# Graph attention with residual and row norm on one core: moving the finish of one late block, and merging two early stores

## The chip, the cores and the metric

The kernel runs on one core of one Trainium2 chip. The metric is the device time in microseconds (us) from the start to the end of one execution. Before the change it is 244.12 us, the median of 4 runs that lie between 243.44 and 244.42 us.

## The reference

`x` is 4096 x 512, `adj` is 4096 x 4096, and there are H = 4 attention heads with a weight W of 512 x (4 * 512).

```python
ht = (h @ W).reshape(N, N_HEADS, N_HIDDEN).transpose(1, 0, 2)
src = jnp.einsum('hnd,hd->hn', ht, a_src)
dst = jnp.einsum('hnd,hd->hn', ht, a_dst)
e = jax.nn.leaky_relu(src[:, :, None] + dst[:, None, :], SLOPE) + adj_mat[None]
att = jax.nn.softmax(e, axis=-1)
h_prime = jnp.einsum('hij,hjd->hid', att, ht)
...
x = _layernorm(x + h_prime.mean(axis=0), axis=-1)
```

The entries of `adj` are zero or reach up to 1e9, so in each row the largest entry outweighs all others in the softmax, as long as it leads the second largest by more than the scores can differ. The attention of a row is then 1 at one column j, and the row's result is the layer norm of `x[i] + x[j] @ mean_h(W_h)`.

## The kernel before

**Work and tiles.** The function `leading_rows` does all of the work in the usual case. Row number `p * 32 + ib` of the matrix is partition `p` of block `ib`, so the 4096 rows make NB = 32 blocks of 128 rows. All of `x` (later the result) is kept in one tile, `hold`, of 128 x 32 x 512 floats. The loop `for t in range(NB)` loads block t of `adj` (2 MB) five steps ahead, takes the maxima of 64 segments of 64 columns on VectorE (DVE), has GpSimd (POOL) fetch the leading segment by an indirect DMA (`lead`), finds the leading column in it two steps later (L193), and has POOL fetch the row of `x` at that column by another indirect DMA (`y`, L181). Three steps later TensorE (PE) transposes this row block (`turn`), ScalarE (ACT) copies it out of PSUM, and PE multiplies it by the mean of the four head weights (`products`, L221) on top of the residual. ACT takes the sum and the sum of squares (`stats`), and two blocks at a time are normalised (`rstd`, then `finish`, L261).

**Three kinds of blocks.** With Q = 4, LATE is 28 and BEHIND is 24. Blocks 0 to 23 are finished inside the loop and held in `hold`; their stores wait until all loads are issued. Blocks 24 to 27 are put by without their residual in a free `adj` buffer (`put_by`), and their `x` is added after the loop (`add_x`). Blocks 28 to 31 come through by the latest data: 28, 29 and 30 by `finish_last`, 31 by `finish_in_halves`. `finish_last(ib, True)` is one chain: DVE adds the residual (L294), takes statistics (L297) and aggregates them (L299), ACT takes the square root (L301), DVE the reciprocal (L302), and DVE scales the block (L303). `rstd_late(26..27)` is a chain for the factors of two blocks: DVE multiply-add (L254), ACT square root (L255), DVE reciprocal (L256) and DVE multiply (L257); then ACT applies the factors in `finish(26)` and `finish(27)` (L261). `finish_in_halves(31)` has two statistics on DVE (L279), an aggregate (L281), a square root on ACT (L283), a reciprocal (L284) and two scalings (L286).

**What sets the order.** The kernel is written under `manual_schedule`: each engine carries out its instructions in the order in which the program lists them, and waits at each for what it needs. The order after the loop (L443 to L492) is written out by hand. Loads of `x`, loads of `adj` and stores all go through the SyncE (SP) queue, in order; each DMA of SP also waits until the one eight places earlier has landed. The indirect DMAs go through POOL's queue, on the same 16 DMA engines. At the end, `report` puts a flag of bad rows in `any_bad` (L393), and all engines branch on it past a general path that isn't taken here.

Of the kernel before, what the change touches and what calls it, by code (L numbers as in the profile page):

```python
# [26 lines left out]
def gat_resnorm_kernel(  # L27
# [29 lines left out]
    any_bad = keep.tile([1, 1], I32, name="any_bad")  # L57

    leading_rows(tc, x, adj, W, a, out, ident, v, n_bad, any_bad)

    flag = nc.values_load(any_bad[0:1, 0:1], min_val=0, max_val=N)
# [5 lines left out]
def leading_rows(ctx, tc, x, adj, W, a, out, ident, v, n_bad, any_bad):  # L67
# [8 lines left out]
    nc = tc.nc  # L76
    N, D = x.shape
    H = a.shape[0]
    KB, NB, S = D // P, N // P, N // E
    AHEAD = 5  # L80
    Q = 4
    PIECES = 4
    LATE = NB - Q
    BEHIND = LATE - Q
# [30 lines left out]
    def load_x(lo, n):  # L115
        nc.sync.dma_start(hold[:, ds(lo, n), :], x_rows[:, ds(lo, n), :])
# [135 lines left out]
    def rstd_late(i):  # L252

        nc.vector.tensor_scalar(sd[:, i], sd[:, i], 1.0 / D, EPS, op0=OP.mult, op1=OP.add)  # L254
        nc.scalar.activation(sd[:, i], sd[:, i], AF.Sqrt)  # L255
        nc.vector.reciprocal(sd[:, i], sd[:, i])  # L256
        nc.vector.tensor_mul(nm[:, i], nm[:, i], sd[:, i])  # L257

    def finish(ib):
        i = slice(ib, ib + 1)  # L260
        nc.scalar.activation(hold[:, ib, :], o_ps.pop(ib), AF.Identity, bias=nm[:, i], scale=sd[:, i])  # L261
# [6 lines left out]
    def products_of_half(ib, k):  # L268
        for kb in range(KB):
            nc.tensor.matmul(  # L270
                o_ps[ib][k], yt_of[ib][:, kb, :], w_sum[:, kb, ts(k, D // 2)],
                start=False, stop=(kb == KB - 1),
            )
# [16 lines left out]
    def finish_last(ib, residual):  # L290

        o = o_ps.pop(ib)
        if residual:
            nc.vector.tensor_add(hold[:, ib, :], o, hold[:, ib, :])  # L294
            o = hold[:, ib, :]
        st = small.tile([P, nc.vector.BN_STATS_DIM], F32, name="st", bufs=2)
        nc.vector.bn_stats(st, o)  # L297
        mv = small.tile([P, nc.vector.BN_AGGR_DIM], F32, name="mv", bufs=2)
        nc.vector.bn_aggr(mv, st)  # L299
        r = small.tile([P, 1], F32, name="r", bufs=2)  # L300
        nc.scalar.activation(r, mv[:, 1:2], AF.Sqrt, bias=eps)  # L301
        nc.vector.reciprocal(r, r)  # L302
        nc.vector.tensor_scalar(hold[:, ib, :], o, mv[:, 0:1], r, op0=OP.subtract, op1=OP.mult)  # L303

    def store(queue, lo, n):
        queue.dma_start(out_rows[:, ds(lo, n), :], hold[:, ds(lo, n), :])
# [93 lines left out]
    for t in range(NB):  # L400
# [24 lines left out]
        ib = t - PROJECT  # L425
# [16 lines left out]

    for ib in range(BEHIND, NB, 2):  # L443
        load_x(ib, 2)
    for ib in range(0, BEHIND, 2):
        store(nc.sync, ib, 2)
    find_column(NB - 2)
    find_column_in_row(NB - 1)
# [33 lines left out]
    products(NB - 2, KB - 1, KB)  # L482
    products_of_half(NB - 1, 0)
    products_of_half(NB - 1, 1)
    rstd_late(slice(BEHIND + 2, LATE))
    finish_last(NB - 2, True)
    finish(BEHIND + 2)
    finish(BEHIND + 3)
    for ib, n in ((NB - 4, 1), (NB - 3, 1), (BEHIND, 2), (NB - 2, 1), (BEHIND + 2, 2)):
# [156 lines left out]
```

## Time and profile before

| What | Value |
|---|---|
| Time, median of 4 runs | 244.12 us (243.44 to 244.42) |
| The profiled execution's own time | 245.29 us |
| Its span, first to last instruction | 243.7 us |
| Mean granted TensorE clock | 0.941 |
| Busy: PE, DVE, ACT, POOL | 201.3, 189.1, 112.1, 96.2 us |
| DMA | 97.73 MB, mean 401 GB/s |
| Stores of two blocks (512 KB), issue to landing, median | 11.8 us |
| Stores of one block (256 KB), issue to landing, median | 2.9 us |

A line of the timeline gives the start of an instruction in us from the start of the span, its duration in us, its engine, its line in the kernel, its operation, what it writes and reads, and, in brackets, how long the engine sat idle before it and what released it. "SPq" is an instruction that issues a DMA. An engine overlaps two of its own instructions a little where neither waits for the other.

### The profile page before, as it was taken

To read this page: it belongs to the slowest core of one execution; us is meant where nothing else is said; L and a number is where in the kernel's file an instruction comes from. 1 tells how busy PE (TensorE), PEld (TensorE's weight loads), DVE (VectorE), ACT (ScalarE), POOL (GpSimd) and SP (SyncE) were. 2 spreads that over 40 slices of the span, in tenths; PEclk is the share of its full clock that TensorE was granted. 3 is DMA by queue.
4 is the path that set the end of the run, shared out by engine and by line. 5 is a ranking of instruction groups with operands and counts; after the bars stand their busy time and mean duration, and the time that the engine had idled before them with its cause. 6 is when DMAs were issued, how large, how long until landed. Compare 5 with 4: busy or idle time off the path is not lost.

```text
span 243.7 us, 2510 instructions
## 1 busy us (share of the span) xinstructions
PE 201.3 (83%) x679; PEld 104.1 (43%) x679; DVE 189.1 (78%) x312; ACT 112.1 (46%) x270; POOL 96.2 (39%) x209
## 2 busy tenths in 40 slices
PE   0198959999999999999959979599949988887950
PEld 0034514755555555555424433243323434433540
DVE  2635785589679886999589969895999999979553
ACT  2002002255656565656645555337524663183961
POOL 1112322334625643645254636363546474441100
PEclk9999776999999999999988999889986999999995
DMA  6999999999999999999999999999999999999944
GB/s 243 432 420 422 420 433 414 427 426 416 420 422 423 407 434 417 425 408 437 415 425 416 428 426 416 416 423 420 424 415 403 408 406 407 411 414 415 383 154 175
DMA packets 14993, 97.73 MB, mean 401 GB/s; under 512 B 2296, under 2 KB 2296, under 8 KB 10240
## 3 DMA queue, kind: packets, MB, share of 16 engines
q1 hardware_dynamic: 11376, 88.09, 87.2%
q0 software_dynamic: 3584, 9.44, 9.8%
q8 instruction: 6, 0.10, 0.2%
q14 instruction: 11, 0.09, 0.1%
q10 hardware_dynamic: 16, 0.02, 0.0%
HBM read 89.15 MB, written 8.39 MB: 400 GB/s over the span
## 4 chain that ended last, share of the span: by engine, by line


## 5 line engine op out<-in xcount | busy, mean ns | idle before, releaser
L158 DVE TENSOR_REDUCE seg<-adj_t 128x32 f32<-128x2048 f32 (+1 forms) x74 | 146.3, 1987 | 38.4 <-DMA adj_t<-in_adj_dram 38.2
L221 PE MATMUL o<-w_sum,yt 128*128 128x512 f32 x248 | 118.9, 621 | 4.2 <-ACT yt L210 4.2
L221 PEld LDWEIGHTS o<-w_sum,yt 128*128 128x128 f32 x248 | 46.5, 198 | 59.9 <-issue 46.6
L210 ACT COPY yt<-tp 128x512 f32<-128x512 f32 x32 | 18.8, 588 | 50.5 <-PE tp L208 50.4
L181 POOL DMA_INDIRECT y<-in_x_dram,col x32 | 30.8, 962 | 18.0 <-POOL col L195 14.6
L171 POOL DMA_INDIRECT lead<-in_adj_dram,row x32 | 32.2, 1006 | 14.2 <-POOL row L169 14.2
L311 PE MATMUL o<-hold,ident 128*128 128x512 f32 x32 | 22.1, 856 | 15.7 <-DMA hold<-in_L_gnn_W_dram 15.7
L208 PE MATMUL tp<-ident,y 128*128 128x128 f32 x128 | 20.0, 280 | 10.4 <-DMA y<-in_x_dram,col 10.4
L214 PE MATMUL o<-hold,ident 128*128 128x512 f32 x48 | 26.2, 629 | 0.0
L208 PEld LDWEIGHTS tp<-ident,y 128*128 128x128 f32 x128 | 15.2, 143 | 21.5 <-issue 21.4
L195 POOL TENSOR_TENSOR col<-start,within 128x1 uint32<-128x1 uint32 x31 | 5.9, 190 | 46.6 <-DVE within L193 46.6
L329 ACT COPY wt<-tp 128x512 f32<-128x512 f32 x16 | 9.2, 588 | 31.4 <-PE tp L327 31.4
L169 POOL TENSOR_TENSOR row<-at,first 128x1 uint32<-128x1 uint32 x32 | 6.1, 190 | 41.0 <-DVE at L167 41.0
L311 PEld LDWEIGHTS o<-hold,ident 128*128 128x128 f32 x32 | 8.4, 275 | 26.9 <-POOL row L169 11.4
L228 ACT ACTIVATE sq<-hold 128x512 f32<-128x512 f32 x32 | 19.8, 620 | 0.0
L335 PEld LDWEIGHTS pv<-at_d,wt 128*128 128x128 f32 x128 | 16.3, 191 | 6.8 <-ACT wt L329 4.0
L312 ACT ACTIVATE w_sum<-o 128x512 f32<-128x512 f32 x4 | 2.4, 597 | 35.3 <-PE o L311 35.3
L261 ACT ACTIVATE hold<-o,nm,sd 128x512 f32<-128x512 f32 x24 | 17.3, 771 | 0.0
L245 ACT ACTIVATE sq<-o,nm 128x512 f32<-128x512 f32 x24 | 16.5, 688 | 0.8
L335 PE MATMUL pv<-at_d,wt 128*128 128x2 f32 x128 | 15.3, 244 | 0.6 <-ACT wt L329 0.6
L243 ACT ACTIVATE sq<-o 128x512 f32<-128x512 f32 x24 | 14.6, 608 | 0.0
L327 PEld LDWEIGHTS tp<-ident,hold 128*128 128x128 f32 x64 | 7.9, 142 | 7.1 <-issue 7.1
(87 smaller groups left out, 135.5 us busy)
## 6 DMA issues: line engine op xcount, KB each, us to landing
adj_t<-in_adj_dram SPq DMA_DIRECT2D x27, 2048.0 KB, 32.5
adj_t<-in_adj_dram SPq DMA_DIRECT2D x20, 512.0 KB, 12.0
out_dram<-hold SPq DMA_DIRECT2D x14, 512.0 KB, 11.8
hold<-in_x_dram SPq DMA_DIRECT2D x6, 1024.0 KB, 33.7
hold<-in_L_gnn_W_dram SPq DMA_DIRECT2D x4, 1024.0 KB, 17.7
hold<-in_x_dram SPq DMA_DIRECT2D x4, 512.0 KB, 11.9
out_dram<-hold SPq DMA_DIRECT2D x4, 256.0 KB, 2.9
lead<-in_adj_dram,row POOLq DMA_INDIRECT x32, 6.2
```

What stands on the lines that cost most here:

```text
L158: nc.vector.tensor_reduce(seg_of[ib][:, ts(k, S // n)], adj_t[ib][:, ts(k, N // n)].rearrange("p (s e) -> p s e", e=E), axis=AX.X, op=OP.max,)
L171: nc.gpsimd.indirect_dma_start(out=lead, out_offset=None, in_=adj_segs, in_offset=bass.IndirectOffsetOnAxis(ap=row[:, :1], axis=0),)
L181: nc.gpsimd.indirect_dma_start(out=y, out_offset=None, in_=x, in_offset=bass.IndirectOffsetOnAxis(ap=col[:, :1], axis=0),)
L208: nc.tensor.transpose(tp[:, kb, :], y[:, ts(kb, P)], ident)
L210: nc.scalar.copy(yt, tp)
L214: nc.tensor.matmul(o_ps[ib], ident, hold[:, ib, :], start=True, stop=False)
L221: nc.tensor.matmul(o_ps[ib], yt_of[ib][:, kb, :], w_sum[:, kb, :], start=(start and kb == 0), stop=(kb == KB - 1),)
L228: nc.scalar.activation(sq, hold[:, ib, :], AF.Square, accum_out=xx[:, ib : ib + 1])
L245: nc.scalar.activation(sq, o, AF.Square, bias=nm[:, i], accum_out=sd[:, i])
L261: nc.scalar.activation(hold[:, ib, :], o_ps.pop(ib), AF.Identity, bias=nm[:, i], scale=sd[:, i])
L311: nc.tensor.matmul(o, ident, hold[:, w_at + kb * H + h, :], start=(h == 0), stop=(h == H - 1))
L335: nc.tensor.matmul(pv[:, kb, h : 2 * H : H], wt[:, k, :], at_d[:, k, h : 2 * H : H], start=(k == 0), stop=(k == KB - 1),)
```

## The change

There are two edits, both in the part after the loop. In the first, blocks 0 to 3 are stored by one DMA of 1 MB in place of two of 512 KB. In the second, the instructions of `finish_last(30)` are listed ahead of those of `rstd_late(26..27)`, in place of after them. The order of the stores stays as it is.

```diff
     for ib in range(BEHIND, NB, 2):
         load_x(ib, 2)
-    for ib in range(0, BEHIND, 2):
+    store(nc.sync, 0, Q)
+    for ib in range(Q, BEHIND, 2):
         store(nc.sync, ib, 2)
...
     products_of_half(NB - 1, 0)
     products_of_half(NB - 1, 1)
+    finish_last(NB - 2, True)
     rstd_late(slice(BEHIND + 2, LATE))
-    finish_last(NB - 2, True)
     finish(BEHIND + 2)
     finish(BEHIND + 3)
```

## The prediction

> **What bounds the kernel now.** First the page's second part. For most of the span the DMA engines are full, and the last slices are not: there the end hangs on a chain of small steps. The page's chain of waits is empty for this run, so I follow the chain by hand in the timeline.
>
> ```profile
> DMA  6999999999999999999999999999999999999944
> GB/s 243 432 420 422 420 433 414 427 426 416 420 422 423 407 434 417 425 408 437 415 425 416 428 426 416 416 423 420 424 415 403 408 406 407 411 414 415 383 154 175
> DMA packets 14993, 97.73 MB, mean 401 GB/s; under 512 B 2296, under 2 KB 2296, under 8 KB 10240
> ```
>
> Both edits lie in the last 38 us. The timeline of DVE at the end (start, duration, line, idle time before):
>
> ```profile
> 232.08 0.14 DVE L393 TENSOR_SCALAR any_bad<-total 1x1 int32<-1x1 f32 x1
> 233.98 0.17 DVE L254 TENSOR_SCALAR sd<-sd 128x2 f32<-128x2 f32 x1 [1.75 <-ACT sq L245]
> 234.41 0.17 DVE L256 RECIPROCAL sd<-sd 128x2 f32<-128x2 f32 x1 [0.27 <-ACT sd L255]
> 234.61 0.16 DVE L257 TENSOR_TENSOR nm<-nm,sd 128x2 f32<-128x2 f32 x1
> 234.69 0.69 DVE L294 TENSOR_TENSOR hold<-o,hold 128x512 f32<-128x512 f32 x1
> 235.42 0.69 DVE L297 BATCH_NORM_STATS2 st<-hold 128x6 f32<-128x512 f32 x1
> 236.15 0.18 DVE L299 BATCH_NORM_AGGREGATE mv<-st 128x2 f32<-128x6 f32 x1
> 236.69 0.16 DVE L302 RECIPROCAL r<-r 128x1 f32<-128x1 f32 x1 [0.36 <-ACT r L301]
> 236.89 0.55 DVE L303 TENSOR_SCALAR hold<-hold,mv,r 128x512 f32<-128x512 f32 x1
> 237.35 0.76 DVE L279 BATCH_NORM_STATS2 st<-o 128x6 f32<-128x256 f32 x2
> 238.14 0.21 DVE L281 BATCH_NORM_AGGREGATE mv<-st 128x2 f32<-128x12 f32 x1
> 238.72 0.16 DVE L284 RECIPROCAL r<-r 128x1 f32<-128x1 f32 x1 [0.36 <-ACT r L283]
> 238.91 0.99 DVE L286 TENSOR_SCALAR hold<-o,mv,r 128x256 f32<-128x256 f32 x2
> ```
>
> DVE stands for 1.75 us, because L254 waits for ACT's sums of block 27; from there to 239.90 it is DVE's chain that ends last. ACT beside it:
>
> ```profile
> 233.76 0.19 ACT L245 ACTIVATION_READ_ACCUMULATOR sq<-hold,nm 128x1 f32 x1
> 234.18 0.20 ACT L255 ACTIVATE sd<-sd 128x2 f32<-128x2 f32 x1 [0.23 <-DVE sd L254]
> 236.36 0.29 ACT L301 ACTIVATE r<-mv,eps 128x1 f32<-128x1 f32 x1 [1.98 <-DVE mv L299]
> 236.56 1.50 ACT L261 ACTIVATE hold<-hold,nm,sd 128x512 f32<-128x512 f32 x2
> 238.39 0.29 ACT L283 ACTIVATE r<-mv,eps 128x1 f32<-128x1 f32 x1 [0.32 <-DVE mv L281]
> ```
>
> ACT is idle for 1.98 us ahead of block 30's root, and finish(26), finish(27) are queued behind that root, though their factors are there at 234.77. The store of block 31 is issued next:
>
> ```profile
> 239.94 0.33 SPq L306 DMA_DIRECT2D out_dram<-hold  x1
> ```
>
> From that issue to the end of the span are 243.7 - 239.94 = 3.76 us (the landing and the closing barrier).
>
> Two rows of the stage before it matter for the merged store: the DMA load where the held blocks are stored (busy time of PE, PEld, DVE, ACT and POOL, granted clock, DMA share, GB/s), and the wait of PE for block 30's rows.
>
> ```profile
> 206.00:218.00 12.00, 10.54 (x31) 4.90 (x30) 10.55 (x18) 5.00 (x13) 4.94 (x11) 1.00 1.03 412
> ```
>
> ```profile
> 224.10 0.63 PE L208 MATMUL tp<-ident,y 128*128 128x128 f32 x4 [1.44 <-DMA y<-in_x_dram,col]
> ```
>
> **The moved finish, step by step.** It adds and removes no instruction. I place each start by the distances above: L294 to L297 and L297 to L299 are 0.73 each, L299 to L301 0.21, L301 to L302 0.33, L302 to L303 0.20, L254 to L255 0.20, L254 to L256 0.43, L256 to L257 0.20. An instruction that waits for nothing starts 0.07 to 0.10 before the end of the one ahead of it.
>
> - L294 follows L393, which ends at 232.22: 232.15. Its operand is there: PE's last product of block 30 ends at 231.1 (the timeline has two of 0.59, from 230.10 on). L297 232.88, L299 233.61.
> - L301 is wanted at 233.82. ACT's sums of block 27 end at 233.95, so it starts at about 233.85. The cover fits almost exactly: the wait costs 0.03.
> - L302 234.18, L303 234.38 to 234.93.
> - L254, now behind these, 234.84 (before: 233.98, so 0.86 later); L255 235.04, L256 235.27, L257 235.47 to 235.63.
> - finish(26), freed by L257, 235.66; finish(27) 0.71 later, 236.37 to 237.17 (before: to 238.07).
> - Block 31's statistics follow L257 at once: 235.54, 1.81 earlier than 237.35. PE ends its halves at 234.7, so they don't wait. L281 is 0.79 later, 236.33.
> - Block 31's root L283 is wanted 0.25 later, at 236.58, but on ACT it is now behind finish(27), which is what is late next: it starts 0.10 before that ends, 237.07. The new wait is 0.49; DVE waits for it, and so does the last store.
> - L284 237.40, L286 237.59 to 238.58, store of block 31 at 238.62: 239.94 - 238.62 = 1.32 us earlier.
>
> Of DVE's 1.81 us, ACT's queue takes 0.49. Bounds: 1.81 if the root should not have to wait, and 1.1 if the small waits at L301, L254 and L283 come out 0.2 dearer together.
>
> The moved step issues no DMA; its store is still the fourth of the last six, now issued at about 234.95 (before: 237.47), ahead of the one of blocks 26 and 27 at 237.19. That 512 KB take 1.27 us at 412 GB/s, and the last store comes 1.43 us after it, so it finds the queue free as it does now (1.85 us). If that cover failed, it would cost 0.2. SP's and POOL's other instructions keep their places. The 3.76 us behind the last issue stay.
>
> **The merged store.** One DMA issue of SP (0.33 us) goes. At 206 SP waits for landings, not for issue time, so this is worth 0. The queue is full: share 1.03, 412 GB/s. The Trainium skill (DMA: Bandwidth & Descriptors, section Bandwidth) advises at least 1 MiB per DMA, and by its fit (2.0 us and bytes at 436 GB/s) two of 512 KB would take 6.4 us and one of 1 MB 4.4: 2.0 us gained, by a transfer that stands alone. Here eight are in flight, and the row shows no gap to fill, so I take 0. Each of the next seven stores waits for a landing one place earlier in the queue and is issued 1 to 2 us sooner; the engines still serve the bytes in the same order, and all loads are ahead of the stores.
>
> There is a rule against the change. The same page (section Queues, rings and completion order) says that a DMA engine takes turns between its queues packet by packet, so a gather waits for one whole packet of SP's queue at each turn. Packet sizes can be read from the page: 14993 - 10240 = 4753 packets have 8 KB or more, and that is 27 adj loads x 128 rows, ten 1 MB loads x 128, and 17 packets of code (the queues' lines list 6 and 11). So a four-block DMA moves in 8 KB packets, a two-block one in 4 KB. At 412 GB/s over 16 engines these are 318 and 159 ns. The merged store is due on the engines at about 213 to 219, where `lead` of block 30 is in flight: issued 209.10, it landed at 214.75, and DVE sat 1.17 us waiting for it. Behind it hang block 30's `y`, issued 216.03, PE's 1.44 us of waiting and the whole end. A `lead` transfer has one row and one semaphore write per engine: at most two turns, each 0.16 longer, 0.32. By the rows, nearest first: `lead` takes 5.6 us among 4 KB packets (206 to 218) and 6.2 as the page's median, mostly among 16 KB packets, so 0.6 for 12 KB more and 0.2 for 4 KB more. The engine that lands last is then still at the 4 KB loads ahead of the store, so I take 0.1, with 0 and 0.35 as bounds. By the 1 MB rule the sum would be -1.3 - 2.0 = -3.3, by the turns rule at its worst -1.0; by the rows -1.32 + 0.1 = -1.2.
>
> **Sum.** The profiled execution would take 245.29 - 1.2 = 244.1 us, with a span of 242.5. Median: 244.12 - 1.2 = 242.9. The profiled run is 1.17 above the median; what makes it longer (if it is block 30's `y`, which took 7.9 us against 6.4 for the one before it) is ahead of all that moves, so the difference should carry over.
>
> **The rivals.**
> - *The gain is swallowed in the ACT queue.* If finish(27) or the root behind it comes 0.7 or more later than placed (a wait for factors, a collision of the last two stores), the gain is below 0.6 and the time is 243.5 to 244.2. Against it: every distance was taken from these same instructions. Chance 0.14.
> - *The merged store delays the gathers.* One mechanism: larger packets in the turns at 213 to 222 delay `lead` and then `y` of block 30. Dearest price by rows: `lead` 6.2 instead of 5.6, and `y` 8.3 (its median over the kernel, mostly among 16 KB packets) instead of 6.4, on top of what `y` of block 30 loses already, together 2.5 us, net 244.1 - 1.3 + 2.5 = 245.3. It is slower by over 0.3% once the delay is over 1.3 + 0.73 = 2.0 us. Against it: the merged DMA is only 8 packets per engine, done by 219, while `y` of block 30 is on the engines after 220. Chance 0.06.
> - *The reorder only exchanges places*, because DVE's chain is as long as before. Against it: the 1.75 us stand empty in the trace and L294's inputs are there. This would be 244.1 and is within the first rival's chance.
>
> **Numbers.** Likeliest, 0.80: 242.9, by its bounds (1.8 to 0.8 gained) 242.3 to 243.3. A measurement tells 0.3%, 0.73 us, from no change: faster means below 243.4, slower above 244.9. Range for 8 in 10, with the spread of the medians (the runs before lie 1 us apart): 242.2 to 243.7. Faster 0.80, same 0.14, slower 0.06.
>
> **What would show it.** Right: L294 of block 30 within 0.1 us after L393; L254 about 0.9 later relative to L393; L301 without a long wait; L283 starting as finish(27) ends, some 0.5 us after L281's end; the last store 6.5 us after L393 instead of 7.86. For the merge: DMA share still about 1 from 206 to 218, `lead` of block 30 still at 5.6 us. Wrong: a wait ahead of L294; PE waiting for `y` of block 30 clearly longer than 1.44 us; or a span that ends over 4 us after the last store's issue.

## The result and the profile after

The changed kernel takes 243.29 us as the median of its runs, the kernel before 244.2 us in the same comparison: a ratio of 0.9962 (95% interval 0.9945 to 0.998), which is 0.9 us less (0.5 to 1.3). The forecast was 1.2 us less. Its profiled execution has a span of 241.0 us, 2.7 us less than that of before. But 1.42 us of these lie ahead of L393, the first row of the timeline below, and are not the change's doing; the last section says where they come from.

DVE at the end of the changed kernel (the timeline's columns as before):

```profile
230.66 0.14 DVE L393 TENSOR_SCALAR any_bad<-total 1x1 int32<-1x1 f32 x1
230.74 0.69 DVE L294 TENSOR_TENSOR hold<-o,hold 128x512 f32<-128x512 f32 x1
...
232.94 0.55 DVE L303 TENSOR_SCALAR hold<-hold,mv,r 128x512 f32<-128x512 f32 x1
233.41 0.16 DVE L254 TENSOR_SCALAR sd<-sd 128x2 f32<-128x2 f32 x1
233.90 0.17 DVE L256 RECIPROCAL sd<-sd 128x2 f32<-128x2 f32 x1 [0.33 <-ACT sd L255]
234.10 0.16 DVE L257 TENSOR_TENSOR nm<-nm,sd 128x2 f32<-128x2 f32 x1
234.18 0.75 DVE L279 BATCH_NORM_STATS2 st<-o 128x6 f32<-128x256 f32 x2
234.96 0.21 DVE L281 BATCH_NORM_AGGREGATE mv<-st 128x2 f32<-128x12 f32 x1
236.03 0.16 DVE L284 RECIPROCAL r<-r 128x1 f32<-128x1 f32 x1 [0.86 <-ACT r L283]
236.23 0.99 DVE L286 TENSOR_SCALAR hold<-o,mv,r 128x256 f32<-128x256 f32 x2
```

Block 30's addition starts 0.08 us after the flag, with no wait. The idle 1.75 us of before are gone, and L254 waits for nothing. The one new stall is 0.86 ahead of L284 (0.36 before). Its cause is in ACT's timeline of the same run:

```profile
232.43 0.28 ACT L301 ACTIVATE r<-mv,eps 128x1 f32<-128x1 f32 x1
233.66 0.20 ACT L255 ACTIVATE sd<-sd 128x2 f32<-128x2 f32 x1 [0.95 <-DVE sd L254]
234.29 1.52 ACT L261 ACTIVATE hold<-hold,nm,sd 128x512 f32<-128x512 f32 x2 [0.43 <-DVE nm L257]
235.72 0.28 ACT L283 ACTIVATE r<-mv,eps 128x1 f32<-128x1 f32 x1
```

Block 31's root (L283) follows finish(27) without a gap, 0.76 after L281 in place of 0.25. The last store is issued here:

```profile
237.25 0.33 SPq L306 DMA_DIRECT2D out_dram<-hold  x1
```

That is 6.59 us after L393 (forecast 6.54, before 7.86): 1.27 us won in the chain. When L393 itself comes differs from execution to execution: before at 232.08, here at 230.66, and in e2 and e3 below, which have the same stores up to there, at 233.16 and 230.90.

The page's count of packets shows the merged store:

```profile
DMA packets 14849, 97.73 MB, mean 406 GB/s; under 512 B 2280, under 2 KB 2280, under 8 KB 9968
```

14849 - 9968 = 4881 packets of 8 KB or more, 128 more than the 4753 of before: the store of four blocks does move in 8 KB packets.

### The profile page after: what moved, and what is told of

The parts are those of the page before. It is cut to its first block, busy times and chain, and to the rows that moved or that the text cites. A ratio compares the mean times of both kernels' runs of the same rounds, so it can differ in the third digit from the quotient of the medians.

```text
span 241.0 us, 2509 instructions
## 1 busy us (share of the span) xinstructions
PE 196.7 (82%) x679; PEld 101.7 (42%) x679; DVE 189.0 (78%) x312; ACT 112.2 (47%) x270; POOL 96.3 (40%) x209
## 2 busy tenths in 40 slices
DMA packets 14849, 97.73 MB, mean 406 GB/s; under 512 B 2280, under 2 KB 2280, under 8 KB 9968
## 4 chain that ended last, share of the span: by engine, by line
issue 34%; POOL 32%; DMA 19%; DVE 5%; PE 4%; ACT 3%; POOLq 1%; SPq 1%; DVEq 0%; ACTq 0%
DMA adj_t<-in_adj_dram 16%; POOL lead L171 11%; POOL y L181 10%; POOL sd L249 4%; DMA y<-in_x_dram,col 3%; PE o L221 3%; POOL start L176 2%; POOL col L195 2%; POOL row L169 2%; DVE seg L158 2%; ACT hold L261 1%; POOL sd L248 1%; POOL nm L250 1%; PE tp L208 1%; DVE col L201 1%
## 5 line engine op out<-in xcount | busy, mean ns | idle before, releaser
L221 PE MATMUL o<-w_sum,yt 128*128 128x512 f32 x248 | 114.9, 604 | 4.2 <-ACT yt L210 4.2
L221 PEld LDWEIGHTS o<-w_sum,yt 128*128 128x128 f32 x248 | 44.8, 191 | 57.0 <-issue 43.7
L311 PE MATMUL o<-hold,ident 128*128 128x512 f32 x32 | 21.0, 818 | 15.6 <-DMA hold<-in_L_gnn_W_dram 15.6
L214 PE MATMUL o<-hold,ident 128*128 128x512 f32 x48 | 25.5, 613 | 0.0
L208 PEld LDWEIGHTS tp<-ident,y 128*128 128x128 f32 x128 | 14.7, 143 | 25.4 <-issue 24.4
```

The costliest lines, as they stand in the source:

```text
L208: nc.tensor.transpose(tp[:, kb, :], y[:, ts(kb, P)], ident)
L214: nc.tensor.matmul(o_ps[ib], ident, hold[:, ib, :], start=True, stop=False)
L221: nc.tensor.matmul(o_ps[ib], yt_of[ib][:, kb, :], w_sum[:, kb, :], start=(start and kb == 0), stop=(kb == KB - 1),)
L311: nc.tensor.matmul(o, ident, hold[:, w_at + kb * H + h, :], start=(h == 0), stop=(h == H - 1))
```

## The experiments

My theory after the result: the moved finish brings all of the gain, by 1.27 us in DVE's chain, and part of it is lost again later. The rivals: the merged store brings a part of it, or costs a part.

**One part alone.** e1 is the change without the merged store, e2 the merged store alone, e3 the changed kernel again, all on one chip.

```diff
 e1, against the kernel before
-    rstd_late(slice(BEHIND + 2, LATE))
     finish_last(NB - 2, True)
+    rstd_late(slice(BEHIND + 2, LATE))
 e2, against the kernel before
-    for ib in range(0, BEHIND, 2):
+    store(nc.sync, 0, Q)
+    for ib in range(Q, BEHIND, 2):
```

> Only finish_last(30) is moved; the stores of blocks 0 to 3 stay two DMAs. My theory: the whole gain is the move. The last store is issued 6.5 to 6.6 us after L393 (7.86 before, 6.59 in the changed kernel), and the time is 0.8 to 1.3 us below the kernel before (ratio 0.9947 to 0.9967), equal to the changed kernel within 0.3 us or up to 0.4 us faster than it if the merged store costs something. Rival (the merge brings part of the gain, by getting the gathers of the last blocks in sooner): ratio 0.998 or above here.

> Only the merged store; finish_last(30) stays behind rstd_late. My theory: 0 to 0.4 us slower than before (ratio 1.000 to 1.0016), with lead of block 30 landing up to 0.4 us later after its issue than the 5.65 us of before, and the last store 7.8 to 7.9 us after L393. Rival (the merge gains): ratio 0.998 or below.

> The changed kernel as it is, on the same chip as the other three, for a second profile of it. My theory: ratio 0.995 to 0.998; the last store 6.6 us after L393 again. The span from the last store's issue to the end of the trace was 3.76 us before and 3.75 here would mean that the transfer at the end costs nothing more; the time of L393 itself moves by a us or more from run to run with the landing of block 30's y. If the shorter tail makes the last transfers collide, as a rival has it, the last store's landing is again longer than before (2.8 against 2.3 us).

Ratios to the kernel before: e1 0.9975 (0.9957 to 0.9993), e2 1.0003 (0.9982 to 1.0025), e3 0.9988 (0.9959 to 1.0017). The move alone makes the kernel faster; the merge alone can't be told from no change, and any part of the gain that it brings is under 0.5 us. e1 and e3 gained less than I had expected. e3 and the first comparison are of the same kernel; weighted by their intervals they put the gain of the change at 0.8 us (0.4 to 1.1), and e1's 0.6 (0.2 to 1.0) lies within it. In the traces the last store is issued 6.59 after L393 in e1 and e3, and 7.86 in e2: the chain's gain is the same in every run. What differs is the stretch from that issue to the end of the trace: 3.72 before and 3.31 in e2, but 3.74 after, 4.33 in e1 and 4.02 in e3. It has two pieces, and each edit changes one of them.

The first piece is the landing. A store lands in sixteen parts, as many as there are DMA engines, and the last part of the last store lands 2.34 us after its issue before and 2.36 in e2, but 2.78 after, 2.96 in e1 and 3.07 in e3. With the move it is later, so some of the 1.27 us is given back there.

The second piece, from that landing to the end, is 1.38 us before and 1.37 in e1, but 0.96 after and 0.95 in e2 and e3. Here the merge saves 0.42 us. SP's DMAs use eight semaphores in turn, and at the end SP waits for them in a fixed order, one wait every 0.06 us. With 79 DMAs on SP (before, e1) seven more waits stand behind the one for the last store; with 78 (the merge) that wait is the last. So SP, which comes to it later, waits less for the same landing; first before, then e2 (us in total, times, longest):

```profile
SPq L641 <- DMA out_dram<-hold: 0.6, 1, 0.6
```

```profile
SPq L642 <- DMA out_dram<-hold: 0.2, 1, 0.2
```

All fourteen profiles keep to it: 0.95 or 0.96 us from the landing to the end with no wait behind, 1.02 with one (e6), 1.14 with three (e7), 1.37 or 1.38 with seven. The interval of e2's ratio is too wide to show these 0.42 us in the time, or to tell whether a delay of the gathers eats them up. So my theory held for the chain, but not for the end of the span: there the merge does bring something.

The merge does hold up a gather, but not the one that I had named. I take the time from issue until fifteen of a transfer's sixteen parts had landed (some traces lack a few parts; then it is the last but one that was recorded). For `y` of block 29 it is 6.24 before, 6.20 in e1; 6.99 after, 7.09 in e2, 6.95 in e3. `lead` of block 30 has 5.56 before and 5.42, 5.26 and 5.24 in the kernels with the merge.

**Packet size and the clock.** e4 stores the held blocks eight at a time, in 16 KB packets.

```diff
 e4, against the changed kernel
-    store(nc.sync, 0, Q)
-    for ib in range(Q, BEHIND, 2):
-        store(nc.sync, ib, 2)
+    for ib in range(0, BEHIND, 2 * Q):
+        store(nc.sync, ib, 2 * Q)
```

> The moved finish stays, and the 24 held blocks are stored by three DMAs of eight blocks (2 MB, rows of 16 KB) in place of one of four and ten of two. It doubles what I suspect of the merge and spreads it over all the time in which lead and y of blocks 30 and 31 are in flight. If larger packets hold up the gathers (the rule of turns by packet), lead of block 30 takes 6.2 us or more and y of block 30 or 31 about 8 us, PE waits longer for y of block 30, and the time is 1.0 to 2.5 us above the changed kernel. If packet size is no matter, it equals the changed kernel within 0.4 us.

Ratio 1.0075 (1.0048 to 1.0101): slower than before although the move is in it, and 2 to 3 us above the changed kernel. On fifteen parts, `y` of blocks 29, 30 and 31 took 8.58, 8.53 and 8.41 us (before 6.24, 6.51, 6.67). So larger packets make the gathers longer. A `y` transfer has 64 packets of data and 16 semaphore writes, so four and one to an engine; if each of the five waits for one packet of SP's, 12 KB more (0.48 us at the stage's 412 GB/s) would make 2.4 us, and 2.0 to 2.3 are seen for the first two. The wait that this makes on PE:

```profile
219.38 0.88 PE L208 MATMUL tp<-ident,y 128*128 128x128 f32 x4 [2.12 <-DMA y<-in_x_dram,col]
```

Then comes something the forecast had no line for. Busy times of PE, PEld, DVE, ACT and POOL, granted clock, DMA share and GB/s by stretch of e4:

```profile
218.00:220.00 2.00, 0.62 (x4) 0.51 (x4) 2.00 (x2) 0.00 (x0) 0.00 (x0) 0.90 1.03 434
220.00:222.00 2.00, 1.32 (x4) 0.55 (x3) 1.39 (x3) 1.70 (x5) 0.95 (x1) 0.50 0.92 387
222.00:224.00 2.00, 2.00 (x4) 0.96 (x3) 1.64 (x5) 0.30 (x3) 0.00 (x0) 0.50 1.05 434
224.00:226.00 2.00, 2.00 (x3) 0.47 (x2) 0.37 (x1) 0.00 (x0) 0.00 (x0) 0.50 1.03 434
```

After PE's idle stretch the granted clock falls to 0.50 for 6.8 us, and the passes of block 29's products come every 0.86 us in place of 0.43. e2 has the same fall (2.13 us idle ahead of block 29). e8 keeps PE busy in that place:

```diff
 e8, against e4, in turn()
         tp = psum.tile([P, KB, P], F32, name="tp", bufs=2)
+        for _ in range(2 if ib == NB - 3 else 0):
+            nc.tensor.matmul(tp.rearrange("p k c -> p (k c)"), ident, hold[:, 0, :], start=True, stop=True)
```

> The kernel with eight blocks to a store, with two additional matrix products (128x512, their result is overwritten) on PE right ahead of the transposes of block 29, where PE sat idle for 2.1 us and the granted clock then fell to 0.50 for some 6 us. If that fall costs what the rows say (six passes of 0.86 in place of 0.43 us, about 2.5 us), the clock now stays at 1.00 from 218 to 226 and turn(30) starts at about 223.5 to 226 as y of block 30 lands (226.2 there); since y of block 30 itself is late with 16 KB packets, the gain in time may be small: 0 to 1.0 us. If the clock makes no difference to the end, the time is that of the kernel with eight blocks within 0.3 us.

```profile
218.00:220.00 2.00, 1.71 (x7) 0.61 (x5) 1.97 (x2) 0.08 (x1) 0.00 (x0) 1.00 1.01 426
220.00:222.00 2.00, 1.44 (x4) 0.73 (x5) 0.93 (x3) 1.92 (x6) 0.94 (x1) 1.00 1.03 432
222.00:224.00 2.00, 1.51 (x5) 0.41 (x3) 1.96 (x6) 0.00 (x0) 0.00 (x0) 1.00 1.01 424
```

The clock stays at 1.00 in this profile, and the ratio is 1.0047 (1.0025 to 1.0069) against 1.0075. The intervals overlap, so what the fall costs is not shown. turn(30) starts at 224.91 in place of 226.43, but that is no measure of it: both times it follows the landing of `y` of block 30, at 224.78 in e8 and at 226.22 in e4, where a code packet had held one part of it up.

**Where the gain is given back.** Three attempts at the end of the run.

e5 is e1 with block 31's root ahead of finish(27):

```diff
 e5, against e1
     finish(BEHIND + 2)
-    finish(BEHIND + 3)
-    for ib, n in ((NB - 4, 1), (NB - 3, 1), (BEHIND, 2), (NB - 2, 1), (BEHIND + 2, 2)):
+    for ib, n in ((NB - 4, 1), (NB - 3, 1), (BEHIND, 2), (NB - 2, 1)):
         store(nc.sync, ib, n)
     finish_in_halves(NB - 1)
+    store(nc.sync, BEHIND + 2, 2)
     store(nc.sync, NB - 1, 1)
...
 in finish_in_halves
         nc.scalar.activation(r, mv[:, 1:2], AF.Sqrt, bias=eps)
+        finish(BEHIND + 3)
         nc.vector.reciprocal(r, r)
```

> The kernel with only the moved finish, and in it block 31's square root listed ahead of finish(27) (the store of blocks 26 and 27 is still ahead of block 31's in the queue). If the new wait is ACT's queue, as placed in the forecast (L283 wanted 0.25 after L281 but held up 0.5 by finish(27)), L283 now starts 0.25 after L281, the last store is issued 6.1 us after L393 in place of 6.59, or as late as finish(27) lets its own store go (6.0 to 6.2). Time 0.2 to 0.5 us below the kernel with only the moved finish (ratio to before 0.993 to 0.997). Rival (the end is set by the last transfers, not by the issue): the issue comes 0.4 earlier, but the stretch from it to the end grows by as much, and the time stays.

L283 starts 0.25 after L281 and the last store is issued 6.10 after L393, as placed: the ACT queue is the cause of the new wait. But the ratio is 0.9988 (0.9971 to 1.0004), no better than e1, and from the issue to the end there are 5.09 us, 0.76 more than in e1. The last part of the last store lands 3.71 us after its issue (2.96 in e1), and even the fourteenth only after 2.76 (2.02 in e1). The 512 KB of blocks 26 and 27 are now issued only 0.53 us ahead of the last store, and at the 1.27 us of the forecast take longer than that to move. The rival was right: with finish(27) delayed, the transfers set the end.

e6 is the changed kernel without the store of blocks 26 and 27, whose rows stay unwritten.

```diff
 e6, against the changed kernel
-    for ib, n in ((NB - 4, 1), (NB - 3, 1), (BEHIND, 2), (NB - 2, 1), (BEHIND + 2, 2)):
+    for ib, n in ((NB - 4, 1), (NB - 3, 1), (BEHIND, 2), (NB - 2, 1)):
```

> The changed kernel without the store of blocks 26 and 27: their 256 rows of the result are not written. In the runs with the moved finish, 3.74 to 4.33 us lay between the last store's issue and the end, against 3.31 and 3.72 without the move, and fifteen of its sixteen parts landed after 1.9 us, one after 2.8 to 3.1. If that late part comes from the 512 KB just ahead meeting the code packets on one DMA engine, then without them all sixteen land within 2.3 us and the end comes 3.3 to 3.5 us after the issue; time 0.3 to 0.8 below the changed kernel. If the late part comes from code packets alone, or from work left over from the stage before, it stays at 2.8 and the end at 3.7 to 4.3.

Ratio 0.9972 (0.9953 to 0.9991), and 4.00 us from the issue to the end: no gain. Fifteen parts of the last store landed within 2.01 us of its issue, the sixteenth after 2.98. In the changed kernel, e1, e3, e4, e8 and e12 it is fourteen within 2.03 us, one after 2.5 to 2.8 and one after 2.8 to 3.1: two late parts, where the expectations speak of one. Without the 512 KB ahead one of the two is gone, but the later one stays, so my first idea, that those 512 KB are what holds up the end, fell.

The trace shows packets of code (8 KB, in a queue of their own) near the last store. One of them starts 1.0 to 1.2 us after the last store's issue in all moved kernels but e5 and e11 (1.95 and 1.64), while the store's parts move; before and in e2 it starts 1.7 us after the issue, when they are nearly through.

e9 puts work that nobody reads behind the last instructions, so that the branches come later.

```diff
 e9, against the changed kernel, at the end
+    idle = rows.tile([P, D], F32, name="sq")
+    for _ in range(3):
+        nc.scalar.copy(idle, hold[:, 0, :])
+    idle = rows.tile([P, D], F32, name="y", bufs=4)
+    nc.vector.tensor_add(idle, hold[:, 0, :], hold[:, 1, :])
```

> The changed kernel with work added behind its last instructions, read by nobody: three copies of 128x512 on ACT (2.0 us) and one addition of 128x512 on DVE (0.7 us), so that both engines come to the closing branch later. In the runs with the moved finish a code packet of 8 KB went out 1.0 us after the last store's issue, while its parts were moving, and one ACT packet 0.4 ahead of it; without the move the second came 1.7 us after the issue, when the parts were through. If these packets are what makes the last part late, both now come 1.5 us or more after the issue, the sixteen parts land within 2.3 us, and the end comes 3.2 to 3.5 us after the issue instead of 3.74 to 4.33, so that more work makes the kernel 0.3 to 0.7 us faster. If the late part has another cause, the end is where it was, or later by the work added (0 to 0.5 us slower).

ACT's branch moved, from 1.50 us ahead of the last issue to 0.76 behind it, and a code packet with it, from 0.39 ahead to 1.85 behind, 1.1 us after the branch in both. The store of blocks 26 and 27 then landed 2.64 us after its issue, where the changed kernel, e1, e3 and e4 have 3.4 to 3.7. DVE's branch did not move: it came 0.15 ahead of the issue (0.16 in the changed kernel), as if nothing had been added. The other code packet went out 1.05 after the issue, and the last store again had one late part (2.95), not two. Ratio 0.9966 (0.9939 to 0.9994), 3.90 us to the end: no gain to be told. So ACT's packet makes the store of blocks 26 and 27 late, and the earlier of the two late parts of the last store goes with it, but the end hangs on the other part. That the other code packet makes that part late fits every trace, but no run took the packet away. That it belongs to DVE's branch is a guess: it follows that branch by 1.2 us in most of the moved kernels, but by 1.6 in e6, 1.8 in e11 and 2.3 in e5.

**Smaller packets.** e7 is e1 with the held blocks stored one by one (2 KB packets); e10 loads the late blocks of x one by one as well; e11 adds e9's tail to e10; e12 is e1 again, on the chip of e9 to e11.

```diff
 e7, against e1
-    for ib in range(0, BEHIND, 2):
-        store(nc.sync, ib, 2)
+    for ib in range(BEHIND):
+        store(nc.sync, ib, 1)
 e10, against e7
-    for ib in range(BEHIND, NB, 2):
-        load_x(ib, 2)
+    for ib in range(BEHIND, NB):
+        load_x(ib, 1)
```

> The kernel with only the moved finish, and the 24 held blocks stored one by one (rows of 2 KB). If packet size in SP's queue sets how long a gather takes (0.16 us for each 4 KB more and each of five turns: y of block 29 has taken 6.2 with 4 KB packets, 7.0 with 8 KB, 8.6 with 16 KB, on fifteen of its sixteen parts), y of blocks 29 to 31 takes about 5.8 to 6.0 us instead of 6.2 to 6.5, and PE's wait for y of block 30 shrinks by as much: time 0 to 0.5 us below the kernel with only the moved finish. Rival: SP's issue, one per 0.6 us, and eight in flight of 256 KB let the DMA engines run dry (share clearly below 1 from 206 to 226), the stores run into the end, and it is 0.5 to 3 us slower.

> Moved finish, stores of the held blocks one by one, and the late loads of x (blocks 24 to 31) one by one too, so that all SP packets of the held loads and stores have 2 KB. With 2 KB stores alone, y of block 30 took 5.9 instead of 6.45 us on fifteen of its parts, while y of block 29, in flight among the 4 KB loads of x, stayed at 6.45. If packets set the gathers' time, y of block 29 now also falls to about 5.9, PE's idle time ahead of turn(29) gets shorter and the clock falls less often: 0 to 0.6 us below the kernel with 2 KB stores alone (ratio to before 0.992 to 0.995). If not, it equals that one.

> The two before this together: 2 KB packets and the late branch. If the two mechanisms are separate, their gains add: ratio to before 0.990 to 0.994, the last store issued 6.6 us after L393 and the end 3.2 to 3.5 us after the issue. If the late part of the last store is not due to the code packets, it equals the kernel with 2 KB packets.

> The kernel with only the moved finish once more, on the chip of the three above, as their common base: ratio to before 0.996 to 0.9985; last store 6.59 us after L393; the end 3.7 to 4.4 us after the issue.

Ratios: e7 0.9944 (0.992 to 0.9969), e10 0.9957 (0.9935 to 0.9979), e11 0.9965 (0.9945 to 0.9984), e12 0.997 (0.9944 to 0.9996). On fifteen parts `y` of block 30 took 5.94 us in e7 and 5.95 in e10 (6.4 to 6.5 with 4 KB, but for e6, where two code packets met it), and `y` of block 29 fell to 5.93 only in e10 and 5.96 in e11, where the loads ahead of it have small packets too (6.45 in e7). So the mechanism holds in this direction as well. What it is worth is a few tenths of a us, less than these intervals can separate; e7 and e10 are the fastest versions measured, and neither is shown to beat the changed kernel. In e10 and e11 the small stores also end later, and 4.40 and 4.78 us lie between the last issue and the end (the last part lands after 3.03 and 3.41, and with 95 DMAs on SP seven closing waits stand behind it again), so the late branch gained nothing.

## Why the forecast was right, and what it missed

**The moved finish: right, step by step.** Measured from L393, forecast and run: L294 0.07 and 0.08, L301 1.77 and 1.77, L303 2.30 and 2.28, L254 2.76 and 2.75, L257 3.39 and 3.44, L283 4.99 and 5.06, L286 5.51 and 5.57, last issue 6.54 and 6.59. Taking the distances from rows of the same instructions worked to within 0.07 us. The new wait behind finish(27) is there with 0.5 us, as forecast, and e5 confirms its cause.

**The stretch after the issue: the term that was mis-sized.** "The 3.76 us behind the last issue stay" took it as a constant. In this pair of profiles it seems to be one (3.72 before with an unrounded span, 3.74 after), but that is luck: two things that the forecast put at nothing cancel.

- The last part of the last store lands 2.76 to 3.07 us after its issue, in the mean 2.90, in seven profiles with the move (the changed kernel, e1, e3, e4, e8, e9, e12; all that have the changed kernel's order of stores at the end and packets of 4 KB or more); it is 2.34 and 2.36 in the two without the move. So the move gives back about 0.55 of its 1.27 us and keeps 0.7, in line with e1's 0.6 (0.2 to 1.0) and e12's 0.7 (0.1 to 1.4).
- The merge takes one DMA from SP's count, and that takes 0.42 us from the closing waits.

For the change that makes 1.27 - 0.55 + 0.42 = 1.1 us, less what the merge costs the gathers; measured are 0.9 (0.5 to 1.3), and 0.8 (0.4 to 1.1) with e3. The forecast looked only at SP's own transfers after the last issue. It did not ask what else comes sooner when the engines finish sooner (their closing branches, and packets of code), nor in which order SP waits at the end.

**The merged store: a sum near nothing, but from other terms.** The forecast put 0 on the issue and 0.1 us on `lead` of block 30, and e2's ratio of 1.0003 is near that. `lead` was not delayed (on fifteen parts). The 8 KB packets moved from 212.6 to 218.2 in the changed kernel, about when forecast, and `y` of block 29 was in flight then (210.28 to 217.35); the forecast did not name it. It lost 0.7 to 0.9 us, and the five turns at 0.16 us that the rows give make 0.8. In the changed kernel's own profile that loss is just covered: turn(29) starts right behind the products of block 28. Against it stand the 0.42 us of the closing waits, which the forecast did not see either. That the sum came out small was luck in part. The rule of turns packet by packet, which the forecast took from the Trainium skill (DMA: Bandwidth & Descriptors, section Queues, rings and completion order), was the right one to weigh; e4 shows what larger packets cost. The 2.0 us by the same page's fit for a transfer that stands alone did not come, as the full queue said: e2 leaves room for 0.44 at most. (The page gives that fit in its section Anatomy of one DMA, for DMAs issued from GpSimd; these stores are SP's.)

**The rivals.** The slower one is what e4 shows when packets are larger still; its path had no place for `y` of block 29, nor for the fall of the clock. The first rival's place was wrong: ACT's queue took 0.5 us as forecast, and the loss came behind it.

## What to carry to other kernels

When a step is moved into an idle stretch at the end, place every instruction by distances from the same trace; that part can be forecast to a tenth of a us. Then ask what lies behind the last issue, because a gain in the chain is paid out only as far as the last transfer's parts let it. Look there too at the order of the closing waits: one DMA more or less, anywhere in the program, shifted it, and was worth 0.42 us here. When a transfer is merged, look at its packet size and at who takes turns with it: larger packets in a full queue made the gathers of `y` beside them slower here, though no byte was added.

## What the runs showed of the hardware that was not expected

**One code packet can make one gather late.** In the window from 220 to 222 us of the kernel before, the queues are these (packets, MB, share of 16 engines):

```profile
q1 hardware_dynamic: 153, 0.55, 67.6%
q0 software_dynamic: 75, 0.25, 31.6%
q8 instruction: 1, 0.02, 3.0%
```

3.0% of 16 engines for 2 us is one packet that holds one engine for 0.96 us. It is 16 KB of code, and `y` of block 30 was in flight:

```profile
DMA to landing us min/median/max: 7.9/7.9/7.9
```

The packet comes at another time in each execution, and the last part of the gather that it meets lands 1.2 to 1.6 us behind the fifteenth: at 220.8 before (`y` of block 30, 7.9), 209.9 in the changed kernel (block 28, 7.7), 204.7 in e1 (block 27, 7.7), 214.6 in e2 and 215.2 in e3 (block 29, 8.4 and 8.2), 209.8 in e12 (block 28, 7.8). Before, it fell on the gather that PE waits for at 224; in the changed kernel it fell on one with slack. `y` of block 30 landed at 223.96 before and at 222.54 in the changed kernel, and turn(30), 224.10 before, starts there at 222.68:

```profile
222.68 0.63 PE L208 MATMUL tp<-ident,y 128*128 128x128 f32 x4
```

These are the same 1.42 us by which L393 differs, which is why single profiles of the two must not be subtracted. Fifteen of the sixteen parts were not held up, which is why they are the better measure of a transfer.

**The clock can fall after little idling.** The granted clock fell to 0.50 after idle stretches of PE of 2.1 us (e2, e4), but also after 1.7 (e9), 1.3 (e5), 1.2 (e7) and 1.0 (e12), and did not after 1.8 us (e3). The Trainium skill (TensorE: Matmul & The Clock Gate, Part 1) has the clock drop after an idle window of about 3.4 us; these runs show the drop after shorter ones, at no fixed length. What else decides was not tried.
